# Block 2 of a four-block attention kernel: keys first, operand transposes placed behind logits, and the first batch's shifts made ahead of the others

## The chip, the cores and the metric

The kernel runs on one core of a Trainium2 chip. That core has a tensor engine (TensorE, PE in profiles), a vector engine (VectorE, DVE), a scalar engine (ScalarE, ACT), GpSimd (POOL) and a queue that issues DMAs (SyncE, SP). Each works through its own queue in order and waits on semaphores for the others. The metric is device time in microseconds. The time before is 4968.75 us, the median of three runs (4967.11 to 4977.68).

## The reference, cut to what matters

Four transformer blocks run one after another on `x` of shape (4, 1024, 288): batch 4, 1024 tokens, 288 channels, 16 heads of 18 channels. The change lies in the third, called `L2` (block 2, counted from zero). Its self-attention is:

```python
def _fake_quant(x, n_bits, always_zero=False):
    levels = float(2 ** n_bits - 1)
    if always_zero:
        delta = max(x) / levels;  zp = 0.0
    else:
        delta = (max(x) - min(x)) / levels;  zp = round(-min(x) / delta)
    xq = clip(round(x / delta) + zp, 0.0, levels)
    return (xq - zp) * delta

q = _fake_quant(q, 8); k = _fake_quant(k, 8); v = _fake_quant(v, 8)
scores = einsum('bhqd,bhkd->bhqk', q, k) * scale
probs  = softmax(scores, axis=-1)
probs  = _fake_quant(probs, 8, always_zero=True)
out    = einsum('bhqk,bhkd->bqhd', probs, v)
```

The steps (`delta`) are global: one for all queries, one for all keys, one for all values, and one for all probabilities. The step of the probabilities needs the largest probability of the whole block, so the attention has to be done twice.

## The kernel before, in words

`fq_attn` first makes queries, keys and values for all 32 token tiles of 128 (four batches of eight), writes them to memory (`raw`), keeps their extremes, and makes the global steps from these (`global_params`, lines 782 to 804). Then `fq_passes` (line 2855) goes through the logits twice.

The **first pass** (lines 2872 to 2942) finds each row's sum of exponentials and each row's largest exponential.

- `levels(b)` loads a tile of raw values (`in`, three buffers) and makes integer levels of its queries, keys and values, three operations for each: two in `fq_levels` (lines 817 and 818) and one that writes the padded bfloat16 tile `pads` or the values `v` (line 2898). For batch 0 this runs on VectorE, for the others on GpSimd. There are four `pads` buffers.
- `operands(b, j)` turns one tile: eight transposes on TensorE for queries and keys (line 2906) into one bank of PSUM, and one copy on ScalarE into `qk` (line 2909).
- The loop over batch `b`, head group `g` (four groups of four heads) and query tile `qt` (eight) does two pairs of heads in each step. For a pair: `scores_pair` (line 3286) issues four matmuls of 512 columns, ScalarE takes the exponential of each head's 1024 logits and their sum (line 2933), and VectorE takes the maxima of both heads in one reduction (line 2940). There are 4 x 4 x 8 x 2 = 256 such pairs. Exponentials lie in four buffers (`e`), logits in three (`ps`).
- Batch 0 is turned ahead of the loop; tiles of batch `b + 1` are turned during batch `b`, at the steps with `n % 4 == 2`.

Program order is not the order in the queues. A scheduler orders each engine's instructions by when it expects their inputs, so a transpose may be queued ahead of logits that stand before it in the program.

**Between the passes**, `prob_shift` (line 2392) works on all 512 columns of sums and maxima (32 tiles of 16 heads): reciprocal, product, the largest of all (a reduction on VectorE, then an all-reduce over partitions on GpSimd), and then, with a logarithm and an exponential on ScalarE, a shift for each row that makes the second pass's exponential come out in units of the probability step. Each shift is split into three bfloat16 numbers (`parts`). Then come GpSimd's loads of small vectors, a memset of `spad` and two memsets of `kz`.

The **second pass** (from line 3047) needs the shifts inside the queries. `add_shift` (line 2415) does this for one tile: GpSimd copies its three parts into three columns of each head in `spad` (line 2420, three instructions), TensorE turns `spad` (line 2426), and VectorE adds the result to the queries (line 2427). `shifts(b, hf)` does four tiles. `spread(n)` copies the keys of one head group into `kz` with four DMAs. The last pass over the context attention (`fq_tail`) uses `prob_shift` and `add_shift` too.

## Time and profile before

| what | us |
|---|---|
| median of three runs | 4968.75 |
| the profiled execution's own time | 4967.9 |
| its span, first to last instruction | 4966.1 |
| first exponential of the first pass starts at | 1777.66 |
| first maximum starts at | 1779.82 |
| reciprocal after the last maximum starts at | 2352.03 |
| first exponential of the second pass starts at | 2380.73 |
| VectorE busy between 1924 and 2350 | 426 of 426 |

A line of the profile names the source line of the kernel, the engine, the operation, what it writes and reads with the shapes, and how often. In the groups there follow the busy time, the mean length of one and the idle time of that engine just before them, with the engine that ended it. In the timeline the line begins with start and length, and the idle time stands in brackets. In the windows each line gives a stretch, its length, then busy time and number of instructions of PE, PE's weight loads, DVE, ACT and POOL, then TensorE's granted clock (0.5 in this stage), the share of the DMA engines and GB/s.

### The profile page before, as it was taken

The numbers are of one execution on the slowest core, as the hardware profiler recorded it, in microseconds if no ns is written. First come the engines' busy times: TensorE is split into PE (matmuls) and PEld (weight loads), VectorE is DVE, ScalarE is ACT, GpSimd is POOL, SyncE is SP. The second block draws the span as 40 slices with busy tenths as digits, with TensorE's granted clock in tenths as the row PEclk, the third lists the DMA queues.
The fourth block names the chain that finished last, engine by engine and source line by source line (L and its number), as shares of the span: only waits on it lengthen the run. The fifth ranks groups of instructions, "written<-read, shape, count | busy, mean of one in ns | idle before, by whom it ended". The sixth has DMA issues, their size and how long they took to land. (4 is left out here: it accounts for less than half of the span.)

```text
span 4966.1 us, 63954 instructions
## 1 busy us (share of the span) xinstructions
PE 4252.1 (86%) x23291; PEld 1719.8 (35%) x23291; DVE 3001.3 (60%) x6686; ACT 3097.4 (62%) x4374; POOL 1273.1 (26%) x2013
## 2 busy tenths in 40 slices
PE   4999997888898979998798873899998999996676
PEld 2333323455565411100233332455443333322343
DVE  8454254665654589999688778333235455344775
ACT  3776774666652269998888864212114777774796
POOL 1001003443312477100122225111111010004664
PEclk9999998899999955555788785899998999997888
DMA  3000002100001221000000022101000000011000
GB/s 81 3 5 15 15 19 87 47 5 17 3 13 62 103 78 39 8 0 0 24 25 25 23 88 71 36 8 33 1 0 15 7 4 12 16 22 34 12 17 21
DMA packets 135638, 136.00 MB, mean 27 GB/s; under 512 B 69260, under 2 KB 111884, under 8 KB 133648
## 3 DMA queue, kind: packets, MB, share of 16 engines
q1 hardware_dynamic: 134112, 128.13, 8.5%
q0 software_dynamic: 1200, 3.69, 0.3%
q8 instruction: 185, 3.03, 0.3%
q14 instruction: 141, 1.16, 0.1%
HBM read 79.92 MB, written 43.47 MB: 25 GB/s over the span
## 5 line engine op out<-in xcount | busy, mean ns | idle before, releaser
L2031 ACT ACTIVATE e<-ps 128x1024 f32<-128x1024 f32 x1024 | 992.6, 1021 | 382.1 <-PE ps L2021 370.9
L2021 PE MATMUL ps<-qT,kT 32*128 32x512 f32 x4096 | 625.3, 644 | 3.9 <-DVE a L1943 3.7
L2940 DVE TENSOR_REDUCE top<-e 128x2 f32<-128x2048 f32 x256 | 561.9, 2275 | 18.6 <-ACT e L2933 18.6
L1981 PE MATMUL ps<-e,v 128*32 128x512 f32 x4096 | 550.5, 608 | 12.4 <-DVE oT L1992 12.4
L2933 ACT ACTIVATE e<-ps 128x1024 f32<-128x1024 f32 x512 | 534.0, 1369 | 19.5 <-PE ps L3286 10.9
L3335 ACT ACTIVATE e<-ps 128x1024 f32<-128x1024 f32 x512 | 483.5, 1060 | 85.7 <-PE ps L3326 68.4
L3286 PE MATMUL ps<-qk 32*128 32x512 bf16 x1024 | 511.1, 604 | 24.3 <-ACT e L2933 23.1
L1758 POOL TENSOR_TENSOR x<-x,y 128x288 f32<-128x288 f32 x192 | 153.0, 807 | 830.8 <-DVE y L1757 489.9
L3338 DVE TENSOR_SCALAR eb<-e 128x2048 bf16<-128x2048 f32 x256 | 322.0, 1261 | 48.5 <-ACT e L3335 46.2
L2933 ACT ACTIVATION_READ_ACCUMULATOR e<-ps 128x1 f32 x512 | 280.6, 550 | 0.0
L1404 POOL TENSOR_TENSOR h<-h,g 128x288 f32<-128x288 f32 x176 | 141.1, 805 | 505.8 <-ACT h L1401 467.2
L3326 PE MATMUL ps<-qk,kz 64*128 64x512 bf16 x1024 | 227.3, 441 | 44.3 <-ACT e L3335 41.2
L2021 PEld LDWEIGHTS ps<-qT,kT 32*128 32x128 f32 x4096 | 189.0, 184 | 208.1 <-issue 119.3
L2464 PE MATMUL psf<-hT,w 128*128 128x512 f32 x576 | 258.0, 600 | 0.6 <-ACT hT L2456 0.6
L1981 PEld LDWEIGHTS ps<-e,v 128*32 128x32 f32 x4096 | 81.1, 108 | 406.4 <-issue 346.4
L1349 PE MATMUL ps<-idb,q 128*128 128x128 bf16 (+2 forms) x1152 | 110.8, 240 | 128.2 <-ACT q L1333 71.6
L3235 ACT ACTIVATE gl<-psf,bf 128x512 f32<-128x512 f32 x72 | 46.0, 684 | 270.7 <-PE psf L2468 266.4
L3286 PEld LDWEIGHTS <-qk 32*128 32x128 bf16 x1024 | 52.8, 99 | 465.0 <-issue 465.0
L1354 ACT COPY qT<-ps 98x384 bf16<-98x384 bf16 (+3 forms) x256 | 151.6, 642 | 71.6 <-PE ps L1349 71.5
L3239 DVE SCALAR_TENSOR_TENSOR u<-psf,bf,gl 128x512 f32<-128x512 f32 x72 | 51.1, 746 | 211.9 <-ACT gl L3235 211.9
L277 PEld LDWEIGHTS <-qT 98*128 98x128 bf16 (+2 forms) x1344 | 133.4, 103 | 128.3 <-issue 44.5
L1880 POOL TENSOR_TENSOR v<-y,wv1b 128x288 f32<-128x288 f32 x64 | 51.6, 812 | 478.8 <-DVE y L1877 478.8
(487 smaller groups left out, 7799.5 us busy)
## 6 DMA issues: line engine op xcount, KB each, us to landing
raw<-y SPq DMA_DIRECT2D x32, 432.0 KB
in<-raw SPq DMA_DIRECT2D x32, 432.0 KB
kz<-qk SPq DMA_DIRECT2D x128, 64.0 KB
wn<-in_L_wfc SPq DMA_DIRECT2D x12, 432.0 KB
x<-in_x SPq DMA_DIRECT2D x4, 1152.0 KB
vvo<-vt SPq DMA_DIRECT2D x16, 288.0 KB
vo<-vvo SPq DMA_DIRECT2D x4, 1152.0 KB
rawq<-y SPq DMA_DIRECT2D x32, 144.0 KB
```

What stands on the lines that cost most here:

```text
L1354: nc.scalar.copy(qT[:, c0 : c0 + r, j0 * P : (j0 + per) * P].rearrange("p c (a t) -> p a c t", a=per), ps[:width, : per * r * P].rearrange ...
L1758: nc.gpsimd.tensor_tensor(self.x[:, t, :], self.x[:, t, :], y, ALU.add)
L1981: nc.tensor.matmul(acc[i * HP : (i + 1) * HP, :], lhsT=st["v"][:, kt, h * (D + 1) : h * (D + 1) + HP], rhs=es_[i // 2][:, i % 2, :], start ...
L2021: nc.tensor.matmul(pss[i // 2][:, i % 2, :], lhsT=self.row_tile(kT, i)[:, kt * P : (kt + 1) * P], rhs=self.row_tile(qT, i)[:, qh * 512 : ( ...
L2031: nc.scalar.activation(e, ps, AF.Exp, scale=SCALE)
L2464: nc.tensor.matmul(o, lhsT=lhs(i)[:, c, :], rhs=rhs(i)[:, c, :], start=(c == 0), stop=False)
L2933: nc.scalar.activation(e[:, j, :].rearrange("p (a n) -> p a n", a=2), sc, AF.Exp, scale=rstep, accum_out=sums[:, t, h0 + j : h0 + j + 1],)
L2940: nc.vector.tensor_reduce(top[:, t, h0 : h0 + 2], e, AX.X, ALU.max)
L3286: self.nc.tensor.matmul(ps[:, c, :], lhsT=self.row_tile(qT, i)[:, g, qt * P : (qt + 1) * P], rhs=self.row_tile(kT, i)[:, g, c * 512 : (c + ...
L3326: nc.tensor.matmul(pss[i][:, n, :], lhsT=kz[rows, i, kt * P : (kt + 1) * P], rhs=qT[rows, g, qh * 512 : (qh + 1) * 512], start=True, stop= ...
L3335: nc.scalar.activation(e[:, 2 * n : 2 * n + 2, :], ps, AF.Exp, scale=step)
L3338: nc.vector.tensor_scalar(eb, e, MAGIC, MAGIC, ALU.add, ALU.subtract)
```

## The change

- **Batch 0, front.** Keys are loaded three tiles at a time and their levels made on VectorE over all three in one instruction. The queries of batch 0 are made on GpSimd (`first_queries`): one tile ahead of the loop, the others one per step of head group 0. Key tiles are turned two at a time, query tiles one at a time (`operands`, now with a choice of queries or keys). The values of batch 0 are made on GpSimd during the last batch (`first_values`).
- **Order.** `scores_pair` keeps its last matmul in `self.last`, and transposes in the loop are issued under `tc.issue_after(self.last)`, which keeps them behind that matmul in the queue. Batch 1 is turned at every third step from the twelfth on, batches 2 and 3 as before. GpSimd's levels are asked for in single thirds of a tile.
- **Per-batch maxima.** `largest(b)` makes the reciprocal, the product and the maximum of one batch during the next batch's steps 2 and 3, and that of the last batch after the loop.
- **Shifts.** The arithmetic of the shifts is done in two parts, columns of batch 0 and columns of the rest (`log_shifts`), with the first four tiles' `shifts(0, 0)` between them in the program.
- **Buffers.** `kz0` and two `spad` tiles are allocated and cleared ahead of the first pass, and the first `spread(0)` stands at the end of the pass. The second `kz` is cleared between the passes. `add_shift` makes one copy with a rearranged view instead of three.

The diff, cut to its core:

```diff
@@ add_shift
-        for k in range(3):
-            nc.gpsimd.tensor_copy(
-                sp[:, :, D + k : D + k + 1], parts[:, k, t * H : (t + 1) * H].unsqueeze(2)
-            )
+        nc.gpsimd.tensor_copy(
+            sp[:, :, D : D + 3], parts[:, :, t * H : (t + 1) * H].rearrange("p k h -> p h k")
+        )
@@ fq_passes
+            kzs = [gp.tile([P, 2, S], BF16, name="kz0")]
+            spads = [gp.tile([P, H, HP], BF16, name=f"spad{n}") for n in range(2)]
...
+                def first_queries():
+
+                    for j0 in range(0, NTB, 3):
+                        m = min(3, NTB - j0)
+                        y = fetch(0, 0, j0, m)
+                        for j in range(m):
+                            self.fq_levels(y[:, j, :], q, 0, nc.gpsimd)
+                            place(0, 0, j0 + j, y[:, j, :], nc.gpsimd)
+                            yield
...
+                def largest(b):
+
+                    rows = slice(b * NTB, (b + 1) * NTB)
+                    flat = lambda ap: ap[:, rows, :].rearrange("p t h -> p (t h)")
+                    nc.vector.reciprocal(flat(r), flat(sums))
+                    yield
+                    nc.vector.tensor_tensor(flat(top), flat(top), flat(r), ALU.mult)
+                    nc.vector.tensor_reduce(tmx[:, b : b + 1], flat(top), AX.X, ALU.max)
+
+                fq0 = first_queries()
+                next(fq0)
+                for j0 in range(0, NTB, 3):
+                    m = min(3, NTB - j0)
+                    y = fetch(0, 1, j0, m)
+                    self.fq_levels(y, q, 1)
+                    for j in range(m):
+                        place(0, 1, j0 + j, y[:, j, :], nc.vector)
+                    for j in {0: (0,), 3: (2, 4), 6: (6,)}[j0]:
+                        operands(0, 1, j, 2)
+                operands(0, 0, 0, 1)
+                nc.gpsimd.memset(kzs[0], 0.0)
+                for sp in spads:
+                    nc.gpsimd.memset(sp, 0.0)
+                spare = iter(())
-                for j, _ in enumerate(levels(0)):
-                    operands(0, j)
                 for b in range(B):
-                    ahead = levels(b + 1) if b + 1 < B else None
+                    ahead = levels(b + 1) if b + 1 < B else first_values()
...
-                            if ahead:
-                                if n % 4 == 2 and n >= 6:
-                                    operands(b + 1, n // 4 - 1)
-                                if n % 4 == 0:
-                                    next(ahead)
+                            with tc.issue_after(self.last) if n or b else nullcontext():
+                                if b == 0 and g == 0 and qt + 1 < NTB:
+                                    next(fq0, None)
+                                    operands(0, 0, qt + 1, 1)
+                                if b == 0 and n >= 12 and n % 3 == 0:
+                                    both(1, n // 3 - 4)
+                                elif 0 < b < B - 1 and n % 4 == 2 and n >= 6:
+                                    both(b + 1, n // 4 - 1)
+                            if n >= 8 if b == 0 else n % 4 < 3:
+                                next(ahead, None)
...
+            z, u = (tp.tile([P, NT * H], F32, name=k) for k in ("lsz", "lsu"))
+            nc.vector.tensor_scalar(y, y, pd, None, ALU.mult)
+            nc.scalar.activation(z, y, AF.Ln)
+            def log_shifts(c0, c1):
+                yc, zc, uc = (ap[:, c0:c1] for ap in (y, z, u))
+                nc.scalar.activation(uc, zc, AF.Exp, scale=-1.0)
+                nc.vector.tensor_tensor(uc, uc, yc, ALU.mult)
+                nc.vector.tensor_scalar(uc, uc, -1.0, 1.0, ALU.mult, ALU.add)
+                nc.vector.tensor_tensor(uc, uc, zc, ALU.subtract)
+                nc.vector.tensor_scalar(uc, uc, rt, None, ALU.mult)
+                for k in range(3):
+                    nc.vector.tensor_copy(parts[:, k, c0:c1], uc)
+                    if k < 2:
+                        nc.vector.tensor_tensor(uc, uc, parts[:, k, c0:c1], ALU.subtract)
...
             with tops:
-                pd, parts = self.prob_shift(gp, tp, top, sums, step)
+                log_shifts(0, NTB * H)
+                for _ in shifts(0, 0):
+                    pass
+                log_shifts(NTB * H, NT * H)
+                self.watch_range(self.R_MIN, self.R_MAX, flat(r), "wr")
...
+            kzs.append(at.tile([P, 2, S], BF16, name="kz1"))
+            nc.gpsimd.memset(kzs[1], 0.0)
...
-            spread(0)
-            side.append(shifts(0, 0))
-            while side:
-                aside()
@@ scores_pair
-                self.nc.tensor.matmul(
+                self.last = self.nc.tensor.matmul(
...
-                )
+                ).ins
```

## The prediction, made before the changed kernel ran

> **What bounds the stage now.** I read the groups of instructions of the page first, to see what the first pass of block 2 spends; then the windows by quarter of that pass, to see which engine is full; then the timeline at its two ends, because the change works there. Groups (line, engine, out<-in, count | busy us, mean ns | idle before):
>
> ```profile
> L2940 DVE TENSOR_REDUCE top<-e 128x2 f32<-128x2048 f32 x256 | 561.9, 2275 | 18.6 <-ACT e L2933 18.6
> L2933 ACT ACTIVATE e<-ps 128x1024 f32<-128x1024 f32 x512 | 534.0, 1369 | 19.5 <-PE ps L3286 10.9
> ```
>
> The 256 maxima fill VectorE for 562 us. Windows (us; busy per engine):
>
> ```profile
> 1780.00:1924.00 144.00, 133.72 (x339) 21.23 (x340) 133.57 (x61) 133.07 (x259) 118.83 (x132) 0.50 0.14 43
> 1924.00:2066.00 142.00, 140.17 (x354) 22.56 (x353) 142.00 (x66) 142.00 (x273) 67.56 (x74) 0.50 0.07 22
> 2208.00:2350.00 142.00, 124.15 (x248) 12.60 (x245) 142.00 (x66) 134.21 (x253) 0.00 (x0) 0.50 0.00 0
> ```
>
> The third busy column is VectorE. It is full in all quarters but the first. So the pass costs 256 maxima at VectorE's pace, plus what VectorE waits at the front, plus the stretch behind it. Timeline of the front (start, length, and in brackets the idle time before):
>
> ```profile
> 1769.83 1.70 POOL L817 TENSOR_SCALAR in<-in,gqrd 128x288 f32<-128x288 f32 x2 [19.64 <-DMA in<-raw]
> 1775.13 0.61 PE L2906 MATMUL ps<-idb,pads 128*128 128x128 bf16 x4 [3.75 <-POOL pads L2898]
> 1777.66 1.03 ACT L2933 ACTIVATE e<-ps 128x1024 f32<-128x1024 f32 x1
> 1779.82 2.29 DVE L2940 TENSOR_REDUCE top<-e 128x2 f32<-128x2048 f32 x1 [8.12 <-ACT e L2933]
> 1783.49 0.61 PE L2906 MATMUL ps<-idb,pads 128*128 128x128 bf16 x4 [6.23 <-POOL pads L2898]
> 1787.22 2.29 DVE L2940 TENSOR_REDUCE top<-e 128x2 f32<-128x2048 f32 x1 [5.12 <-ACT e L2933]
> 1794.50 2.29 DVE L2940 TENSOR_REDUCE top<-e 128x2 f32<-128x2048 f32 x1 [4.99 <-ACT e L2933]
> ```
>
> TensorE reaches transposes of the *second* batch (L2906) before logits of the first, and they wait for GpSimd. VectorE therefore idles 5.12, 4.99 and, at 1797.11, 0.33 us: 10.4 us inside the pass. The tail:
>
> ```profile
> 2352.03 3.34 DVE L2400 RECIPROCAL rs<-sums 128x512 f32<-128x512 f32 x1
> 2359.45 0.63 ACT L837 ACTIVATE lsz<-lsy 128x512 f32<-128x512 f32 x1 [12.60 <-DVE lsy L835]
> 2360.10 1.28 ACT L840 ACT_TABLE_LOAD   x1
> 2370.16 3.58 POOL L3033 MEMSET kz<- 128x2048 bf16 x2
> 2373.66 0.54 POOL L2420 COPY spad<-parts 128x16 bf16<-128x16 bf16 x3
> 2380.73 18.44 ACT L3335 ACTIVATE e<-ps 128x1024 f32<-128x1024 f32 x20 [18.71 <-PE ps L3326]
> ```
>
> From the last maximum (2352.03) to the first exponential of the second pass (2380.73) there are 28.7 us. The rate inside: (2352.03 - 1779.82 - 10.44) / 256 = 2.194 us for a pair of heads; when not held up, ScalarE and TensorE do a pair in 1.99 us each (20 matmuls in 10.04 us at 1796.12; two exponentials 1797.96 to 1799.95).
>
> **Part 1, the front: -15.9 us.** Before, VectorE makes 72 operations (8 tiles, q, k and v, three each) of 0.28 us from 1750.54 to 1771.6. Now it makes keys alone: two level operations on 864, 864 and 576 columns, and eight placements. The length of a tensor_scalar is 0.36 us for 288 columns and 0.82 for 1152 (L2949), so an estimate for 864 is 0.67, 0.08 less from start to start. In the built order, with the small parameter operations between: first chunk placed at 1753.7, second at 1755.2. The load of the third chunk can be asked for only at 1753.8, when the first chunk's buffer is free. A load of 432 KB showed 3.3 us from a buffer's release (last read of its tile by VectorE at 1766.5) to the GpSimd use at 1769.83; for 288 KB I take 3.0, so 1756.8. Then 0.43 + 0.43 + two placements give 1758.3; transposes (0.61) 1758.95; copy of a 1024-column operand (1.01) 1760.1; copy of the first query tile (512 columns, 0.59 from 0.40 at 288 and 0.48 at 384) 1760.7; logits 1.0 as at 1776.65; first exponential about 1761.8, first maximum 1763.95 against 1779.82.
> The first query tile is cover here: on GpSimd it costs 0.5 + 1.25 + 1.0 (L817, L818, L2898), with a memset of kz (1.8) and one of spad (0.56) queued between, ready near 1756.5, some 2.4 us before it is needed. A rule speaks against that. The Trainium skill, "SBUF — State Buffer", section "Who interferes with whom": while VectorE runs in a two-port mode, which tensor_scalar can enter, GpSimd is blocked for the whole instruction, and the reverse. By the rule in its worst form GpSimd gets nothing until VectorE's pause at 1755.2, the tile comes near 1761, and the front gains about 12. The row: at 1769.83, beside the last VectorE levels, the first L817 took 1.18 us instead of 0.50, and the VectorE operations at 1770.63 and 1771.21 took 0.54 and 0.49 instead of 0.36. Tenths, not a stop; I take the row and keep 12 for the range.
>
> **Part 2, idle time inside the pass: -8.4 us.** Transposes now stand behind the logits before them, so the 10.4 us go, if GpSimd is ahead: 2.75 us for a query tile against 4.39 for VectorE's two pairs, and 8.25 for a whole tile against the 13.2 (six pairs) or 17.6 (eight) between transposes. Values of batch 0 move to the last quarter, where GpSimd has no work (0.00 above): 8 x 2.75 us; hidden, and their loads too. What is new: steps 0 to 6 each add four transposes (0.5 us, half of 1845.18 to 1846.16) to TensorE and a 0.59 copy, about 0.5 from start to start, to ScalarE. With two pairs that makes 4.5 us for each against 4.39, while the four e buffers are still empty. If the two overlap it costs 7 x 0.1, if they add up 7 x 0.6; later ones (1.0 us against six pairs' 1.2 of slack) may add a few us. I take 2, range 0.7 to 8.
>
> **Part 3, work moved under the bound: +3.9 us.** For batches 0 to 2 reciprocal, product and maximum now stand between maxima on a full VectorE: 0.84 + 0.25 + 0.25 (quarters of 3.34, 0.68 and 0.69, with their fixed part) = 1.3, three times. Nothing hides them.
>
> So the last maximum ends at 1763.95 + 561.8 + 2 + 3.9 = 2331.6, 20.4 earlier.
>
> **Part 4, the tail: -11.3 us.** From that moment, in the built order: reciprocal, product, two range maxima of 0.62, two small ones: 2.75 (before 6.2). All-reduce and parameter 0.75, product with 512 sums 0.5. Here comes a wait the old tail did not have: the table load for Ln is now queued with the wait on that product (before it ran at 2345.57, hidden), so 1.28 more; then Ln 0.63 and the Exp table 1.28. The skill's "ScalarE: Activation LUTs", section "Table sets: the hidden batching unit", has Ln then Exp in one set with one load; the rows show a load for each, and I count both (2.6 instead of 1.3). Exp of 128 columns 0.3. The shift arithmetic of batch 0 is interleaved with that of the other three: nine small operations (1.8) with seven of 384 columns (3.0), 4.8 against 5.3. Then GpSimd copies at once: memset of kz, three loads and the rest stood ahead of it from 2367.3 to 2373.66. The first key spread (four DMAs) went out during the pass, so it is not late. Two copies 0.5, TensorE 0.61, third copy; a 1.8 us memset of kz now stands ahead of the fourth copy; copy, transpose 0.61, add 0.42, logits 0.65: 5.0 in all. Sum 17.4 against 28.7. Three g/b/bo loads (0.55 each) and the second spread come after; they are needed a key group, 15 us, later.
>
> **Part 5, one copy instead of three in add_shift: -1.5 us.** In the second context pass TensorE waits 0.49 us per group of four tiles for these copies (0.49 at 3127.85, 0.43 at 3217.01). Three cost 0.53. A 48-column one, bounded by 0.25 (16 columns) and 0.53, I put at 0.34: 7 groups x 0.2 = 1.4, with the start 1.5. Range 0 to 4.
>
> **Sum.** -15.9 - 8.4 + 3.9 - 11.3 - 1.5 = -33.2. Against the profiled execution (span 4966.1, own time 4967.9) 4934.7; against the median 4968.75 it is 4935.5, which I give. Profiled run and median differ by 0.9 us.
>
> **Rivals.** (a) Group 0 becomes the bound: GpSimd is locked out at the front (+4) and transposes and copies add up on TensorE and ScalarE (+6). For it: both run a pair in 1.99 us, only a tenth below VectorE. Against: full VectorE from 1924 on with eight transposed tiles in the window. 4945.5. (b) The front does not start earlier, because the third key load or the query tile is late: the 15.9 go, 4951.4. Against: VectorE never waited for a load before 1771. (c) Slower: the transposes are now fixed in TensorE's in-order queue; if GpSimd's tile is late at each, logits, ScalarE and VectorE wait behind it. There are 7 + 24 = 31 such places; it decides from 33.2 / 31 = 1.07 us each that reaches VectorE. At 1.5 us each: 4968.75 - 33.2 + 46.5 = 4982. For it: the 6.23 us waits above are this. Against: 2.75 against 4.39.
>
> **How the numbers follow.** All parts as worked out: 0.74, own range 4926 to 4943. (a) 0.16, (b) 0.06, (c) 0.04. The range 4924 to 4951 takes in (a), most of (b), and the bounds of parts 1, 2 and 5. A difference of 0.2% (10 us) is about what can be told from none. Faster: 0.74 + 0.16 + most of (b) = 0.94; same 0.02; slower 0.04.
>
> **What would show it.** First maximum 14 to 17 us earlier, at 14 to 16 us after the gqr reduction; VectorE idle between maxima under 8 us; three breaks of 1.3 us; 16 to 19 us from the last maximum to the first exponential of the second pass; waits for spad copies in the last pass halved. The prediction is wrong if TensorE's waits for pads reach VectorE in the first batch, or if the tail stays above 22 us.

## The result, and the profile after

The changed kernel takes 4952.12 us (median of six runs, 4945.58 to 4959.41). The kernel before, run beside it, took 4977.77 us (six runs, 4967.11 to 4984.23). The ratio is 0.9951, interval 0.9936 to 0.9967: faster by 0.5%. Forecast were 4935.5 us with a range of 4924 to 4951, so the median lies just outside. The sign was right, the forecast gain too large: 33.2 us were forecast, the medians measured side by side differ by 25.7, the two profiled spans by 22.3 (4966.1 and 4943.8).

The totals of one and the same kernel scatter by 14 us and more. The stretch that the change touches doesn't, so it is read on its own here, in the one profiled execution of each kernel, in three parts:

- *front*: from the start of the partition reduction of the scales (L791, `gqr`) to the first maximum;
- *pass*: from there to the reciprocal behind the last maximum;
- *tail*: from there to the second pass's first exponential.

| us | front | pass | tail | sum |
|---|---|---|---|---|
| before | 30.45 | 572.21 | 28.70 | 631.36 |
| forecast | 14.58 | 567.65 | 17.4 | 599.6 |
| after | 21.41 | 571.32 | 17.38 | 610.11 |

The tail is as forecast. The front misses 6.8 us, the pass 3.7. That is the whole difference in this stretch: 21.25 us gained against 31.7 forecast.

The groups of the page after (busy us, mean ns, idle before):

```profile
L3025 DVE TENSOR_REDUCE top<-e 128x2 f32<-128x2048 f32 x256 | 563.5, 2274 | 14.2 <-ACT e L3018 14.0
L3018 ACT ACTIVATE e<-ps 128x1024 f32<-128x1024 f32 x512 | 520.5, 1153 | 6.7 <-PE ps L3394 3.3
```

VectorE's idle time before maxima fell from 18.6 to 14.2 us. Of that 9.33 stand ahead of the first, and 4.7 are inside the pass, where there were 10.4 before and 2 were forecast. The windows by batch (PE, weight loads, VectorE, ScalarE, GpSimd):

```profile
1771.40:1914.00 142.60, 129.99 (x346) 21.39 (x346) 142.10 (x65) 141.71 (x275) 114.63 (x126) 0.50 0.15 42
1914.00:2057.00 143.00, 132.98 (x317) 19.31 (x316) 141.41 (x68) 134.96 (x261) 73.69 (x81) 0.50 0.10 29
2057.00:2200.00 143.00, 133.12 (x317) 19.27 (x316) 140.91 (x67) 134.95 (x263) 42.15 (x46) 0.50 0.05 13
2200.00:2343.00 143.00, 125.73 (x250) 12.86 (x249) 142.33 (x69) 132.87 (x255) 0.00 (x0) 0.50 0.00 0
```

The first batch is now nearly full, as forecast. The second and third, full before, are not any more: VectorE lacks 1.6 and 2.1 us there. The timeline of the front:

```profile
1749.97 0.40 POOL L791 PARTITION_ALL_REDUCE gqr<-gqs  x1 [20.15 <-DVE gqs L789]
...
1758.42 0.52 DVE L817 TENSOR_SCALAR in<-in,gqrd 128x576 f32<-128x576 f32 x1 [2.56 <-DMA in<-raw]
1758.60 0.71 POOL L817 TENSOR_SCALAR in<-in,gqrd 128x288 f32<-128x288 f32 x1 [7.82 <-issue]
...
1759.26 2.10 POOL L2992 MEMSET kz<- 128x2048 bf16 x1
1759.73 2.32 DVE L2910 TENSOR_SCALAR pads<-in,gqtop 128x288 bf16<-128x288 f32 x2
1761.36 1.30 POOL L818 TENSOR_SCALAR in<-in,gqnzp 128x288 f32<-128x288 f32 x1
...
1763.13 1.02 POOL L2910 TENSOR_SCALAR pads<-in,gqtop 128x288 bf16<-128x288 f32 x1
...
1766.56 1.02 ACT L3018 ACTIVATE e<-ps 128x1024 f32<-128x1024 f32 x1 [1.12 <-PE ps L3394]
...
1769.75 0.59 ACT L2954 COPY qk<-ps 128x512 bf16<-128x512 bf16 x1 [2.08 <-PE ps L2949]
...
1770.23 1.03 ACT L3018 ACTIVATE e<-ps 128x1024 f32<-128x1024 f32 x1
...
1771.38 4.48 DVE L3025 TENSOR_REDUCE top<-e 128x2 f32<-128x2048 f32 x2 [9.33 <-ACT e L3018]
```

Four things are to be seen. GpSimd begins its first query tile 7.82 us after its last memset, and the profile finds nothing that it waited for ("issue"). The memset of `kz` stands between that tile's operations, and VectorE's placement of two key tiles, which took 0.64 us at 1753.68, takes 2.32 beside it. The third load of keys is there at 1758.4. And the first and second exponential are 3.7 us apart, because a copy (of the *second* query tile) stands between them and waits for GpSimd. The tail:

```profile
2342.70 0.94 DVE L2976 RECIPROCAL rs<-sums 128x128 f32<-128x128 f32 x1
...
2346.72 1.28 ACT L3046 ACT_TABLE_LOAD   x1 [10.49 <-DVE pv L3078]
...
2348.66 1.28 ACT L3051 ACT_TABLE_LOAD   x1
...
2354.67 0.91 POOL L2419 COPY spad<-parts 128x48 bf16<-128x48 bf16 x2 [8.73 <-DVE parts L3057]
...
2356.15 1.80 POOL L3082 MEMSET kz<- 128x2048 bf16 x1
2357.90 0.26 POOL L2419 COPY spad<-parts 128x48 bf16<-128x48 bf16 x1
...
2360.08 3.77 ACT L3443 ACTIVATE e<-ps 128x1024 f32<-128x1024 f32 x4 [9.39 <-PE ps L3434]
```

Both table loads are in the chain and the memset of `kz` stands ahead of the fourth copy, each at the forecast length.

### The profile page after: what moved, and what is told of

It reads as the page before. It is cut to its first block, busy times and chain, and to the rows that moved or that the text cites. A ratio compares the mean times of both kernels' runs of the same rounds, so it can differ in the third digit from the quotient of the medians.

```text
span 4943.8 us, 63809 instructions
## 1 busy us (share of the span) xinstructions
PE 4245.7 (86%) x23291; PEld 1727.7 (35%) x23291; DVE 2986.6 (60%) x6645; ACT 3092.6 (63%) x4379; POOL 1292.3 (26%) x1934
## 5 line engine op out<-in xcount | busy, mean ns | idle before, releaser
L3025 DVE TENSOR_REDUCE top<-e 128x2 f32<-128x2048 f32 x256 | 563.5, 2274 | 14.2 <-ACT e L3018 14.0
L3394 PE MATMUL ps<-qk 32*128 32x512 bf16 x1024 | 499.9, 604 | 40.7 <-ACT e L3018 38.9
L3018 ACT ACTIVATION_READ_ACCUMULATOR e<-ps 128x1 f32 x512 | 172.9, 338 | 0.0
```

Of the source, the lines that this page charges most:

```text
L3018: nc.scalar.activation(e[:, j, :].rearrange("p (a n) -> p a n", a=2), sc, AF.Exp, scale=rstep, accum_out=sums[:, t, h0 + j : h0 + j + 1],)
L3025: nc.vector.tensor_reduce(top[:, t, h0 : h0 + 2], e, AX.X, ALU.max)
L3394: self.last = self.nc.tensor.matmul(ps[:, c, :], lhsT=self.row_tile(qT, i)[:, g, qt * P : (qt + 1) * P], rhs=self.row_tile(kT, i)[:, g, c ...
```

## The experiments

Every experiment edits the changed kernel. This table has them all; the ratio is to the kernel before, run beside each.

| us | front | pass | tail | sum | ratio (95%) |
|---|---|---|---|---|---|
| changed kernel | 21.41 | 571.32 | 17.38 | 610.11 | 0.9951 (0.9936 to 0.9967) |
| first query tile on VectorE | 19.62 | 571.04 | 17.37 | 608.03 | 0.9957 (0.9938 to 0.9975) |
| memsets later | 18.44 | 571.02 | 17.37 | 606.83 | 0.9948 (0.9928 to 0.9967) |
| third key load early | 21.20 | 571.34 | 17.37 | 609.91 | 0.9951 (0.9936 to 0.9966) |
| free transposes | 21.04 | 566.07 | 17.35 | 604.46 | 0.9952 (0.9935 to 0.9969) |
| three edits of the front | 17.01 | 570.75 | 17.37 | 605.13 | one run |
| these and free transposes | 17.14 | 565.82 | 17.38 | 600.34 | 0.9934 (0.9918 to 0.9951) |
| reduction on TensorE | 19.10 | 575.46 | 17.35 | 611.91 | 0.9964 (0.9951 to 0.9977) |
| reduction on TensorE, later memsets, early load, free transposes | 18.34 | 566.59 | 17.36 | 602.29 | 0.9943 (0.9927 to 0.9959) |
| second query tile held | 18.09 | 574.59 | 17.37 | 610.05 | 0.9953 (0.9937 to 0.9968) |
| all of the front, free transposes, held | 14.07 | 568.92 | 17.37 | 600.36 | 0.9932 (0.9918 to 0.9945) |
| largest probabilities at the end | 21.09 | 570.16 | 20.20 | 611.45 | 0.9951 (0.9935 to 0.9966) |
| held behind pairs, zeroed early | 14.06 | 569.42 | 17.36 | 600.84 | 0.9947 (0.9934 to 0.9960) |

Where the reduction is on TensorE, the front is counted from 0.41 us after the start of L789's reduction, which is where L791 starts in the others. The tail repeats to 0.03 us in the twelve kernels that leave it alone. The front scatters more: the two kernels whose edits lie behind it (free transposes, largest probabilities at the end) have 21.04 and 21.09 against 21.41, so a difference of 0.4 us in it shows nothing. The ratios' intervals are 0.3% wide (15 us); so verdicts on a few us are taken from the stretch.

**1. What is GpSimd waiting for?** Theory A: it reloads its code. After each of the partition reductions `kqr`, `gqr`, the first `pdd` and `qqr`, the next tensor_scalar or tensor_tensor in GpSimd's queue comes with an instruction that the trace names `MODIFY_POOL_CONFIG`; memsets and plain copies that stand before it do without. The lines of source L817 in the changed kernel have it right behind the memset of `v`:

```profile
L817 POOLq MODIFY_POOL_CONFIG  x2: 22/22/23, 1750.8 to 1750.8; - x2
```

Theory B: GpSimd is locked out by VectorE on a shared port. The first run gives the first query tile to VectorE:

```diff
-                            self.fq_levels(y[:, j, :], q, 0, nc.gpsimd)
-                            place(0, 0, j0 + j, y[:, j, :], nc.gpsimd)
+                            eng = nc.gpsimd if j0 + j else nc.vector
+                            self.fq_levels(y[:, j, :], q, 0, eng)
+                            place(0, 0, j0 + j, y[:, j, :], eng)
```

> One edit to the changed kernel: the first tile of queries is levelled and placed by VectorE, not by GpSimd. 'Front' below is the time from the start of the partition reduction of the scales (L791, gqr) to the first maximum: 30.45 us before, 21.41 us in the changed kernel. Theory A (library switch): after the partition reduction GpSimd reloads its library when the first tensor operation comes up in its queue, and this takes the 7.8 us that stand as 'issue' before its first L817. In this kernel's queue the memsets of kz and spad come ahead of it, so GpSimd's first L817 (second query tile) comes not earlier but later, near 1762 on the changed kernel's clock, and its place near 1766; the first exponential comes at about 1765 (third key load 1758.4, then placements, transposes, copy, logits), the second at about 1768 because the copy of the second query tile is queued ahead of it. Front 19 us, total 2.4 us below the changed kernel. Theory B (port shared with VectorE): GpSimd starts as VectorE runs out of work, near 1758.6 or a little later for VectorE's 1.2 us more; second exponential near 1766, front 16.5. Theory D (third key load is the whole bound): first exponential at 1764.8, front 18 to 19 whatever GpSimd does.

Front 19.62, where A expected 19 and B 16.5 (D, the late load, expected 18 to 19 too; experiment 3 tests it). VectorE and GpSimd in this kernel:

```profile
1757.75 2.41 DVE L799 TENSOR_SCALAR gqd<-gqd 128x3 f32<-128x3 f32 x1
1757.87 1.81 POOL L2993 MEMSET kz<- 128x2048 bf16 x1
1759.61 1.01 POOL L2995 MEMSET spad<- 128x512 bf16 x2
1767.65 0.98 POOL L817 TENSOR_SCALAR in<-in,gqrd 128x288 f32<-128x288 f32 x2 [7.02 <-issue]
```

The memsets, now ahead of the reload in the queue, run at once and aren't held; the reload's 7.0 us are counted from their end. The tensor operation came 10.5 us after the reduction instead of 8.6, and VectorE had by then been out of work for 1.6 us (from 1766.06). That fits a reload that takes its turn in the queue and not a port. That the sum came out near A's 19 is in part luck: the first line shows a tensor_scalar on the scales, 128 x 3 numbers, that took 2.41 us beside the memsets in place of 0.21, so the first exponential came at 17.0 us after the reduction where A had 15, while the second followed it sooner than A had it. The direct test takes the reduction away from GpSimd, so that nothing has to be reloaded:

```diff
-        nc.gpsimd.partition_all_reduce(
-            r.rearrange("p a m -> p (a m)"),
...
+                nc.tensor.transpose(a[:k, :P], s.rearrange("p a m -> p (a m)"), self.idf)
+                nc.vector.tensor_reduce(mk, a[:k, :P], AX.X, ALU.max)
+                nc.vector.tensor_scalar(dg, self.idf[:k, :k], mk, None, ALU.mult)
+                nc.tensor.matmul(c[:, :k], lhsT=one, rhs=dg, start=True, stop=True)
+                nc.vector.tensor_copy(r.rearrange("p a m -> p (a m)"), c[:, :k])
```

> One edit to the changed kernel: the six scales' maxima over the partitions are taken by TensorE (a transpose, a reduction, a small matmul that spreads them) and VectorE, not by GpSimd's partition reduction, so that GpSimd has no library to reload ahead of its query tiles. Front from the start of the last reduction of the scales (L789 in the changed kernel, 21.82 us to the first maximum there). The scales come an estimated 1.5 us later (five short instructions of about 0.2 to 0.4 in place of one). Theory A: GpSimd's first tensor operation follows the scales at once, within 1 us or right after the memset of kz, not 7 to 8 us after; the first query tile is placed before the third keys, which bound the first exponential: keys arrive 10.4 us after the start, placed at 12.6 to 13.6, transposes, copy and logits 2.8: first exponential 15.4 to 16.4, second 1.0 later, first maximum at 17.6 to 18.6. Theory B (port shared with VectorE): GpSimd's first tensor operation still starts at 8 to 10 us, when VectorE has run out of work, and the front stays at 21 to 23.

```profile
1753.05 1.80 POOL L3006 MEMSET kz<- 128x2048 bf16 x1
1753.58 1.29 DVE L801 TENSOR_SCALAR gqdg<-idf,gqmk 6x6 f32<-6x6 f32 x1
1756.43 0.96 POOL L831 TENSOR_SCALAR in<-in,gqrd 128x288 f32<-128x288 f32 x1 [1.58 <-DVE step L2863]
...
1803.73 127.30 DVE L3039 TENSOR_REDUCE top<-e 128x2 f32<-128x2048 f32 x58 [4.73 <-ACT e L3032]
```

GpSimd's first tensor operation follows the scales (ready at 1756.33) within 0.1 us: the 7.8 us are gone with the reduction, and so is L817's `MODIFY_POOL_CONFIG`. So it is shown that the reduction brings the delay, as A had it. That the time goes into loading code is a reading of the instruction's name, and of the page cited below. The front gains 2.3 us although the scales come 2.5 us later than in the changed kernel (3.31 us after the start of L789's reduction, 0.84 there). From L789 it is 0.9 us longer than the top of the forecast, and one cause stands in the second line: a product of 6 x 6 numbers took 1.29 us and ended at 1754.87, as the memset of `kz` did (1754.85). So B exists too, here between a GpSimd memset and a VectorE tensor_scalar, and not where the 7.8 us were. The last line says more: the pass lost 4.1 us, more than the front won, in a stall of 4.73 us ahead of the thirteenth maximum, the first one of query tile 6 (0.35 us in the changed kernel). There TensorE stood 5.43 us on a transpose of a query tile that GpSimd had not placed yet; GpSimd itself had waited 3.81 us, until 1771.84, for its second load of queries, and made values of the next batch in between (1790.67 and 1797.93). Such stalls are taken up in 5.

The Trainium skill, "GPSIMD Engine Reference", section "Instruction dispatch", says that the first call into freshly loaded code costs about 6 us with no instruction to be seen. This chip shows 7.0 to 8.2 us at this place over these kernels; the measurement decides, and the page names the mechanism.

**2. GpSimd's own queue.** The memsets of `kz` and both `spad` go to the second batch in the program:

```diff
-                nc.gpsimd.memset(kzs[0], 0.0)
-                for sp in spads:
-                    nc.gpsimd.memset(sp, 0.0)
...
+                            if b == 1 and n in (3, 7, 11):
+                                nc.gpsimd.memset((kzs[0], *spads)[n // 4], 0.0)
```

> One edit: the memsets of kz and of both spads are issued in the second batch, out of the first query tiles' way. Theory C (GpSimd's own queue): the first query tile is placed 1 to 2 us earlier (L817 of two tiles 1.0, L818 of two 2.5, place 1.0 after 1758.6: 1763.1 in place of 1764.15, the end of the place), VectorE's third placements lose the 1.6 us by which they were stretched while the memset ran, and the copy of the second query tile is no longer queued ahead of the second exponential: first exponential about 1765.3, second 1766.4, first maximum 1767.5; front 17.5 us, 4 us below the changed kernel. Theory A alone: GpSimd's first L817 still starts 7.8 us after the memset of v, at 1758.6. If the memsets didn't matter: front 21.4.

```profile
1766.63 1.35 POOL L817 TENSOR_SCALAR in<-in,gqrd 128x288 f32<-128x288 f32 x2 [7.85 <-issue]
1767.71 0.95 DVE L2910 TENSOR_SCALAR pads<-in,gqtop 128x288 bf16<-128x288 f32 x2
```

The reload stays (7.85), VectorE's placement takes 0.95 in place of 2.32, and the front falls by 3.0 us, of 4 expected. VectorE's loss beside a memset was thus 1.4 us, and beside GpSimd's tensor_scalar it is 0.3 for these two (0.95 against 0.64). The 1.4 us are not what the front gained, though: the first exponential came only 0.3 us sooner (16.3 us after the reduction for 16.6), as it waits for the query tile. The other 2.7 come from the queue: GpSimd now makes the first two query tiles together, the second one's copy stands ahead of both exponentials, and these follow each other by 1.0 us and not by 3.7.

**3. The third load of keys.** It goes into a buffer of the exponentials and is asked for early:

```diff
+                    if (b, n, j0) == (0, 1, 6):
+                        y = ep.tile([P, 2, S], F32, tag="e", name="e")
+                        y = y.rearrange("p a s -> p (a s)")
+                    else:
+                        y = ld.tile([P, 3 * C], F32, tag="in", name="in")
```

> One edit: the third load of keys goes into a buffer of the exponentials, which is free then, so its request does not wait for the first keys to be placed and the data lie in SBUF before the scales are known. Theory D (late third load): keys are all placed by about 1758 in place of 1762.05, and if that is the bound of the first exponential, it comes 2 to 4 us earlier, front 17.5 to 19.5. Theory A or C (the first query tile is the bound): the query tile is placed at 1764.15 as before, the first exponential moves by under 0.5 us, the second stays behind the copy of the second query tile, and the front stays at 21.0 to 21.4; total within 0.5 us of the changed kernel.

Front 21.20, as expected of A and C. The keys were placed 4.3 us sooner, relative to the reduction, and the front fell by 0.2, which is within its scatter: the load was late, but the query tile was later.

**4. The held transposes.** After the first batch they are free again:

```diff
-                                elif 0 < b < B - 1 and n % 4 == 2 and n >= 6:
-                                    both(b + 1, n // 4 - 1)
+                            if 0 < b < B - 1 and n % 4 == 2 and n >= 6:
+                                both(b + 1, n // 4 - 1)
```

(the two new lines stand outside the `issue_after`).

> One edit: in the batches after the first, the transposes of the next batch's operands are no longer held behind the last logits issued; the scheduler puts them where it likes, as in the kernel before. The changed kernel has 4.7 us of VectorE idle inside the pass (0.35 in the first batch, 1.6 in the second, 2.75 in the third, in pieces of 0.40 to 0.67 at every fourth or so tile of queries that a transposed tile follows). Theory E (the transposes sit on TensorE between the release of a PSUM buffer and the logits that need it): the idle of the second and third batch goes, 4.3 us; pass from first maximum to the last reciprocal 571.3 to about 567. Rival F (ScalarE's sum of exponentials and copies is too long in those batches, whatever the place of the transposes): idle stays at 4 to 5 us. Rival G (with free placement TensorE waits for GpSimd's tiles in its queue): new idle in long pieces, pass over 573. The front stays at 21.4.

Pass 566.07, 5.25 us less. The third batch, ScalarE and VectorE in the changed kernel, then VectorE here:

```profile
2131.85 1.01 ACT L2967 COPY qk<-ps 128x1024 bf16<-128x1024 bf16 x1 [1.05 <-PE ps L2964]
...
2134.92 17.64 DVE L3025 TENSOR_REDUCE top<-e 128x2 f32<-128x2048 f32 x8 [0.52 <-ACT e L3018]
2153.08 17.64 DVE L3025 TENSOR_REDUCE top<-e 128x2 f32<-128x2048 f32 x8 [0.52 <-ACT e L3018]
```

```profile
2080.38 133.87 DVE L3025 TENSOR_REDUCE top<-e 128x2 f32<-128x2048 f32 x61
```

With the hold, VectorE waits 0.52 us once in every eight maxima, which is once for each transposed tile; without it, 61 maxima run without a gap. So the place of the transposes makes the gaps, as E had it: held, they and the copy stand one after the other between two pairs of heads, and ScalarE waits 1.05 us for the transposes before it copies (first line). E's detail, which PSUM buffer is waited for, was not tested. TensorE waited for GpSimd's tiles at the end of the first batch (0.79 and 0.37 us), and none of it reached VectorE: G is out, and so is F.

The price of the hold is hidden in part by other work. The `largest` of the first three batches were put back to the end:

```diff
-                    spare = largest(b)
-                for _ in spare:
-                    pass
+                for b in range(B):
+                    for _ in largest(b):
+                        pass
```

> One edit undone in the changed kernel: the reciprocals and the largest probability of the first three batches (L2976 to L2979) are taken after the last maximum, not inside the pass. Theory V (VectorE is full where they stand, so they cost there what they cost at the end): pass 571.3 minus 3.75 (3 times 0.86 + 0.20 + 0.19) = 567.6, tail 17.4 plus 3.75 = 21.1, total unchanged within 0.5 us, and of the tail's gain of 11.3 us the 3.75 that were counted against the pass are a shift from one place to the other. Rival (they fill idle time of VectorE in the pass): pass falls by less than 1.5, tail rises by 3.75, total 2 us or more above the changed kernel.

```profile
2098.38 17.64 DVE L3025 TENSOR_REDUCE top<-e 128x2 f32<-128x2048 f32 x8 [0.52 <-ACT e L3018]
2116.54 17.64 DVE L3025 TENSOR_REDUCE top<-e 128x2 f32<-128x2048 f32 x8 [0.52 <-ACT e L3018]
```

The pass falls by 1.2 us and the tail rises by 2.8, together 1.3 more than the changed kernel: for the pass the rival expectation was right, for the sum the truth lies between the two. At 2098 and 2116 VectorE had no gap in the changed kernel, since `largest` had put it 1.25 us behind at the start of that batch; now the wait is there at every transposed tile, seven in the third batch, 3.8 us. So part of `largest` runs in time that the held transposes leave free, and the price of the hold with nothing to fill it is an estimated 7.7 us for the two batches (twice 3.8), not the 4.3 that can be seen in the changed kernel.

**5. The sum of the edits, and what took it back.** Three edits of the front together, those of the first query tile, of the memsets and of the third load:

> Three edits together: the first query tile on VectorE, the memsets of kz and spad in the second batch, the third load of keys into a buffer of the exponentials. If the switch of GpSimd's library (theory A), the place of its memsets (C) and, only once these are out of the way, the third load (D) are what held the front, the first exponential now waits for VectorE alone: keys placed 7.7 us after the partition reduction's start (as with the third load's edit alone) plus 1.2 for the query tile, transposes and copies 2.4, logits 1.1: first exponential 12.7, second 13.7, first maximum 14.9 us after it; the second query tile is placed at about 13.2 and its copy stands behind four exponentials. Front 15 us (14 to 16), against 21.4. If one of the three single edits' gains were the same microseconds counted twice (first tile 1.8, memsets 3.0, third load 0.2), the front would stay at 18 or above.

Front 17.01, between the two expectations (15 and 18). The first exponential came at 14.9 us and not at 12.7: the copies it needs were done at 10.8, but the scheduler had queued the second query tile's copy ahead of it. In the changed kernel nothing holds that one back (`if n or b else nullcontext()`); there it lands behind the first exponential, here before it. With free transposes in addition:

> The three edits of the front and the free transposes together. Front 15 us (against 21.4), pass 566 (against 571.3, as with the free transposes alone), tail 17.4: 11.7 us below the changed kernel, about 37 below the kernel before, ratio to it about 0.9926. If the front's earlier tiles only make the first batch run ahead of GpSimd, the gain comes back as idle in the first batch: front 15, pass 568 to 571.

Front 17.14, pass 565.82: the pass as expected, 9.8 us less than the changed kernel in all. And the variant that keeps the first query tile on GpSimd but has no reload:

> The reduction on TensorE, the memsets of kz and spad later, the third load of keys early, and the free transposes; the first query tile stays on GpSimd. From the start of the last reduction of the scales: keys placed at 9.6 plus up to 1 where GpSimd's operations on query tiles run beside VectorE's, transposes and copies 2.1 to 2.5, logits 1.1: first exponential 13.5 to 14.5, first maximum 15.7 to 16.7 (the other combined kernel: 15.4). Pass 566, tail 17.4. Total within 1.5 us of the other combined kernel. If GpSimd without its reload is slowed by VectorE beyond 2 us, first maximum after 18.

(the edits of the reduction, the memsets, the third load and the transposes). Front 18.34, pass 566.59: 2.0 us behind the kernel above, half a microsecond more than expected. The first maximum came 18.75 us after L789's reduction, where 18 had been set as the sign that VectorE slows GpSimd. The trace shows the two slowing each other: VectorE's work on the keys, from its first level operation to the last placement, took 9.07 us here and an estimated 6.2 in the kernel with the three edits (7.06 less three query operations of 0.28 each). So 2.8 us went into operations that run beside GpSimd's, some tenths in each, where up to 1 had been expected.

Then the second query tile is held like the others:

```diff
-                                if b == 0 and g == 0 and qt + 1 < NTB:
+                                if b == 0 and g == 0 and 0 < qt and qt + 1 < NTB:
...
+                            if b == 0 and n == 0:
+                                with tc.issue_after(self.last):
+                                    next(fq0)
+                                    operands(0, 0, 1, 1)
```

> One edit to the changed kernel: the second query tile's transposes, and with them its copy on ScalarE, are held behind the first tile's logits (in the changed kernel that is so from the third tile on; for the second, nothing holds them). Theory H (the second query tile's copy stands in ScalarE's queue between the first and the second exponential, and waits there for GpSimd): the first exponential stays at 16.6 us after the start of the partition reduction, the second follows it by 1.0 and not by 3.7, the first maximum comes at 18.8 in place of 21.4. As the second and third tile's copies then follow the fourth exponential together, up to 0.8 us of idle may come into the pass (571.3 to 572.1). Total 1.8 to 2.6 us lower. Rival: the second exponential waits for something else (its logits, which wait for the first query tile's other half): it stays 3.7 us behind the first, front 21.4.

> The three edits of the front, the free transposes and the held second query tile together. With the three edits alone the first exponential stood 14.9 us after the partition reduction's start, because the scheduler had put the second query tile's copy, which ended 14.4 after it, ahead of it in ScalarE's queue; the copies before that were done at 10.8. Held back, the first exponential comes at 11.9, the second at 12.9, the first maximum at 14.1; the pass takes 565.8 as with the free transposes, or up to 0.8 more for the two copies that then stand behind the fourth exponential. Tail 17.4. That is 2 to 3 us below the kernel with the four edits, 13.5 to 14.5 below the changed kernel. If another wait stands behind the copy (the logits' PSUM buffers, or the first query tile's copy), the front stays at 16 to 17.

H holds: the exponentials follow each other by 1.0 us, the fronts are 18.09 alone and 14.07 with everything (14.1 expected). But the gain came back, to the tenth: 3.3 us less in front and 3.3 more in the pass in the one, 3.1 and 3.1 in the other. In the first it went into 1.25 us and, ahead of the thirteenth maximum again, 2.72, with TensorE 3.43 us on a tile of GpSimd's. Where it went in the second, on TensorE and VectorE:

```profile
1771.56 22.52 DVE L3030 TENSOR_REDUCE top<-e 128x2 f32<-128x2048 f32 x10 [1.25 <-ACT e L3023]
...
1908.51 0.61 PE L2969 MATMUL ps<-idb,pads 128*128 128x128 bf16 x4 [2.83 <-POOL pads L2914]
...
1912.24 11.06 DVE L3030 TENSOR_REDUCE top<-e 128x2 f32<-128x2048 f32 x5 [1.65 <-ACT e L3023]
```

1.25 us where two copies stand together, and 1.65 us where TensorE waits for a tile of GpSimd's, with the logits queued behind. The last run, on top of all these edits, takes both causes on: one copy between two pairs of heads, and `kz` and `spad` zeroed before the phase begins.

```diff
+            for z in (*zeroed[0], *zeroed[1]):
+                nc.gpsimd.memset(z, 0.0)
...
+                                if b == g == pr == 0 and qt + 1 < NTB:
+                                    with tc.issue_after(self.last):
+                                        next(fq0)
+                                        operands(0, 0, qt + 1, 1)
```

> The kernel with the held second query tile and all edits reached its first maximum 14.1 us after the start of the partition reduction, 3.1 sooner than without the hold, and lost the 3.1 again inside the first batch: 1.25 us where the copies of the second and third query tile stand together between two tiles, 1.65 us five maxima before the batch's end, where TensorE stood 2.83 us on a transpose whose tile GpSimd had not placed yet. Here every query tile's transposes are held behind the first pair of heads of the tile before, so that one copy stands between two pairs, and kz and the spads are zeroed when the whole phase begins, so that GpSimd has 2.8 us less to do in the first batch. Theory S (GpSimd's supply of tiles bounds the first batch once it begins early): front 14.1, the idle of 1.25 falls to under 0.3, that of 1.65 goes or falls to under 0.5, pass 566 to 567 in place of 568.9, tail 17.4; from the start of the partition reduction to the second pass's first exponential 597.5 to 598.5 us, against 600.4 with the hold alone and 610.1 in the changed kernel. Rival (another wait takes the same microseconds, as it did twice): 600 or more.

```profile
1795.14 0.61 PE L2959 MATMUL ps<-idb,pads 128*128 128x128 bf16 x4 [2.85 <-POOL pads L2919]
...
1798.90 114.15 DVE L3029 TENSOR_REDUCE top<-e 128x2 f32<-128x2048 f32 x52 [2.15 <-ACT e L3022]
```

The rival won: 600.84. The 1.25 us went down to 0.37 and the 1.65 to 0.92, and a new wait of 2.15 came, again on a tile of GpSimd's (query tile 7). Zeroing early didn't help: GpSimd's queue also has operations of the next batch between the last query tiles (values at 1784.85 and 1793.10). What is shown is that these waits (5.43, 3.43, 2.83 and 2.85 us on TensorE) are for tiles that GpSimd has not placed. They have two kinds. Three are for one of the last query tiles, and there GpSimd is busy all the while, with work of the next batch among it. The 2.83 us stand near the batch's end, in the kernel with everything held, and there GpSimd stood still before it could begin the tile:

```profile
1901.05 0.99 POOL L817 TENSOR_SCALAR in<-in,gqrd 128x288 f32<-128x288 f32 x2 [3.53 <-DMA in<-raw]
```

Nine such waits for loads add up to 26.0 us between 1760 and 1915, and a load is issued only when GpSimd has placed the last part of a tile before (at 1909.46, 0.03 us after a placement's end). So the second kind is a matter of late loads as much as of GpSimd's pace. Neither another order on GpSimd nor earlier loads were tried.

## Why the prediction was off

**Part 1, front: -15.9 forecast, -9.0 measured. This step failed**, in the sentence "The first query tile is cover here [...] ready near 1756.5". It was placed at 1764.15; counted from the start of the reduction that is 14.2 us where the forecast had 7.1, so 7.1 us late. GpSimd's reload alone is 7.8 us (experiment 1), and the forecast didn't list it; the kernel before has its instruction at the same place, hidden in a wait of 19.64 us for a load. It could have been read. In the trace of before, GpSimd stood idle behind the earlier reduction `kqr` (put down there to a VectorE operation, though the tile `h` that it reads was ready at 1644.96):

```profile
1651.31 1.53 POOL L146 TENSOR_TENSOR h<-h,g 128x288 f32<-128x288 f32 x2 [6.88 <-DVE vbd L2792]
```

The page of the Trainium skill cited in experiment 1 has a price for it, too. The 6.8 us that the front misses divide so: the first exponential came 4.16 us later than forecast (16.59 us after the reduction for 12.43), since it waits for that query tile, and the first maximum another 2.67, since the second exponential did not follow at once. A step that moves work up behind another instruction inherits whatever that instruction leaves behind.

The choice between rule and row belongs here. The forecast took "tenths, not a stop" for the port. For a single tensor_scalar beside a tensor_scalar the row held (experiment 2), but the changed kernel hardly tests it, as GpSimd stood in its reload while VectorE worked. Without the reload the tenths added up to an estimated 2.8 us (experiment 5), where the forecast put nothing. For a memset on GpSimd the rule of the Trainium skill ("SBUF — State Buffer", "Who interferes with whom") held in full: 1.4 us in experiment 2, and two short tensor_scalars of 2.41 and 1.29 us in experiment 1. In the changed kernel this cost the front nothing that can be seen, since the query tile came after the keys. The rule's worst form (a gain of 12) still left more gain than the 9.0 that came, since the larger part of the loss came from elsewhere. The third load, forecast 7.4 us after the reduction, came at 8.5; that term was mis-sized by 1.0 us and decided nothing (experiment 3).

The second exponential, forecast to follow the first at once, waited for a copy of the next tile: a queue order that nothing in the program fixed. Holding that copy back closed the gap, and the front fell by 3.3 us (experiment 5).

**Part 2, idle time: -8.4 forecast.** The 10.4 us are gone. The new idle was put at 2, range 0.7 to 8, and measured 4.7 in the changed kernel. The mechanism named for group 0 (transposes and copies add up) can't be seen there: the one gap, 0.35 us, comes with a wait of 1.05 us on TensorE for a tile of GpSimd's. In the second and third batch, which the step passed over with "later ones [...] may add a few us", it costs 0.52 us a tile. There transposes and copy do add up, as rival (a) had it, but in other batches, and only because the hold puts them one behind the other: free, the same transposes and copies leave no gap. The idle accounts for 2.7 of the 3.7 us that the pass misses. The other 1.0 is the pace: less the idle and the three breaks, the 256 maxima took 562.9 us against 561.8 forecast. Without the hold there the pass takes 566.07, 1.6 us below the forecast's 567.65.

**Part 3, largest: +3.9 forecast.** The instructions cost 1.25 us a batch, as worked out. "Nothing hides them" was wrong for the kernel as built: undoing them gave back 1.2 us in the pass and not 3.75, because the held transposes leave time free (experiment 4). Parts 2 and 3 can't be added.

**Part 4, tail: -11.3 forecast, -11.3 measured.** The sum is right to 0.02 us, which is closer than its terms, but the order that it rests on is there: both table loads in the chain and the memset ahead of the fourth copy.

**Part 5, one copy for three: -1.5 forecast.** The time after the tail scatters by more than 10 us between kernels with the same code there, so the effect on the total can't be tested. In the last pass, TensorE's stretch of sixteen transposes shrank from 1.84 to 1.48 us. One of the seven places, first in the kernel before, then in the changed one:

```profile
3215.97 0.61 PE L2426 MATMUL ps<-idb,spad 128*128 128x128 bf16 x8
3217.01 0.80 PE L2426 MATMUL ps<-idb,spad 128*128 128x128 bf16 x8 [0.43 <-POOL spad L2420]
```

```profile
3198.87 0.61 PE L2425 MATMUL ps<-idb,spad 128*128 128x128 bf16 x8
3199.64 0.71 PE L2425 MATMUL ps<-idb,spad 128*128 128x128 bf16 x8 [0.17 <-DVE x L3363]
```

Added up over the seven places, the waits were 3.02 us and are 1.59, 1.4 less, as worked out. At six of the seven GpSimd is no longer what ends the wait; a 48-column copy took 0.26 us, below the 0.34 assumed.

**The rivals.** (b), in which the front doesn't start earlier "because the third key load or the query tile is late", was true by half: the query tile was late and the front lost 6.8 of the 15.9. (c), transposes in TensorE's queue that wait for GpSimd, occurs at two places in the changed kernel (2.58 and 1.05 us) instead of 31. The 2.58 us are the wait behind the late second exponential, so they are part of the front's loss; the 1.05 reach VectorE as 0.35, a small case of the sign that the forecast had named for being wrong. The rival came forward when the front was made faster. The forecast of the whole stretch, 599.6 us, was nearly met by three of the experiments (600.3 to 600.8), but in the sum and not in the parts: with a front of 17.1 us the pass took 565.8, with one of 14.1 it took 568.9 or more. None got below it: with a front of 14 us, GpSimd's supply of tiles is the next bound, which the forecast had excluded by comparing 2.75 us for a tile with 4.39 for VectorE. That rate holds only when GpSimd starts on time, makes nothing else in between and does not wait for its loads.

The best of the kernels tried is 9.8 us below the changed one in this stretch. In the totals its ratio is 0.9934 against 0.9951, with intervals that overlap, so the stretch shows the gain and the totals don't contradict it.

## What to carry to other kernels

When an operation is moved up in a queue, read what stands ahead of it there, including what the instruction before leaves to be done: behind a GpSimd reduction over partitions the next tensor_scalar or tensor_tensor came 7 to 8 us late, so give that first tile to another engine, and keep GpSimd's memsets away from it. Holding filler work behind a matmul keeps it from blocking early; where the scheduler could have placed it freely, the hold cost 0.5 us each time, so hold only the places that need it. And when a front gets shorter, look for the next supplier: here 3 us won in front were paid back within the batch, twice to the tenth.

## What the runs showed of the hardware

- GpSimd's reload after a partition reduction takes 6.9 to 8.2 us, starts when its turn comes in the queue, and doesn't hold memsets queued ahead of it (in the kernel with the first query tile on VectorE 3 us of memsets ran first, the reload's 7.0 us came after).
- A GpSimd memset of 128 x 2048 bfloat16 (1.8 to 2.1 us) stops a VectorE tensor_scalar until it is over, even one of 6 x 6 numbers (1.29 us) or of 128 x 3 (2.41 us for 0.21, with a second memset right behind). GpSimd's float32 tensor_scalar beside VectorE's cost each placement some 0.2 us (1.53 us for three placements in the kernel with the reduction on TensorE, 0.93 in the changed one).
